# Two samples' steps dealt from a table, a gate's convolutions moved to VectorE, shorter checks, and q and k first in the ending

## The chip, the cores and the metric

The kernel runs on one core of a Trainium2 chip. A core has TensorE (PE, matrix products into the eight banks of PSUM), VectorE (DVE), ScalarE (ACT), GpSimd (POOL) and the queues that issue DMAs, here almost all SyncE's (SP). The metric is the device time of one execution in microseconds (us); several executions are made and their median is quoted. The profile is one further execution, taken by the hardware profiler.

## The reference

Sixteen samples x of 256 channels and 32 x 32 pixels, in float32, go through four layers (B the sample, C = 256, N = 1024 pixels):

```python
# layer 0: group norm, attention over pixels, projection, residual
xn = group_norm(x)
q, k, v = split(w_qkv @ xn + b_qkv)
x = w_proj @ (softmax(q.T @ k / sqrt(C)) @ v) + b_proj + x
# layer 1: a spatial gate
m, M = mean(x, channels), max(x, channels)
r = relu(conv3x3([m, M], w1) + b1)
x = x * sigmoid(conv3x3(m + M + r, w2) + b2)
# layer 2: like layer 0, with its own weights
# layer 3: attention with q and k of 32 channels, no norm
e = clip(q.T @ k / sqrt(32), -10, 10)
x = gamma * (softmax(e) @ v) + x
```

## The kernel before, in words

**Products.** The large products are made by Strassen's scheme in Winograd's form: `seven` takes 2 x 2 blocks and makes seven products instead of eight, with sums of blocks made by VectorE and results copied out of PSUM by ScalarE or added by VectorE (L909 plus, L978 and L1227 copies). Every float32 product is two passes on TensorE, so the profile counts two records for each. Weights are folded at the start (`fold`): logits are x^T M x with M from the weights of q and k, and the weights of v and of the projection are one matrix.

**A sample** is a generator, `sample(b)`, which issues a few instructions, yields, and goes on when it is called again. `attend` (layers 0 and 2) makes t = M x (`seven`, 4 yields), values (4), their sums (1), and for each half of the queries logits (8), a pause (2) and weighted values (7): 43 steps. Between layers 0 and 2 come 9 steps of waiting, the gate (`gate_of`, 4), the scaling of each half, its turn by VectorE and its way through DRAM into the channel layout (`turn` L825, `send` L836 and L840; 2), 4 of waiting, and the group norm (16). Then `attend` again, 7 of waiting, and layer 3 (`clipped_attend`, 30). That is 158 steps in all. Layer 3 has q and k by `qk_products` (L1375, on half the array's columns) and scores by `score_products` (L1401, four products at a time on 32 rows each; a group of them fills four banks and is emptied by four exponentials, L1417). A sample visits the scores four times. Even samples are lane 0, odd ones lane 1, each with its own buffers; the tile `t` of a lane holds t, then z (the turned gate result), then layer 3's q and k.

**The gate.** The planes of mean and maximum (pl, 128 x 8) are copied into 32 x 32 rows (L468), which `neighbours` (L458, L459) repeats on 96 partitions, shifted by one pixel. A convolution is then a product with a banded matrix `toep` (L473 for two planes, L490 for their sum). POOL builds `toep` at the start from a table of taps that is loaded (`build_toep`, L397 to L402; `tidx`, L582). The sigmoid is an exponential (L502), a sum and a reciprocal.

**The checks.** The fast path counts conditions on the data and weights in `n_ok`, and a general path runs if one fails. `alike` and `moderate` square weights, sum them over partitions by products with ones (L1103, L1147, L1157) and compare the extremes.

**The order.** Three generators are dealt out by a rule: `stream(0)` and `stream(1)` run even and odd samples one after another, and `later` holds the rest of the preparation (the head of sample 1, the folding of layers 2 and 3, `toep`, the checks). For `OFFSET` = 30 turns stream 0 alternates with `later`; after that the two streams alternate, `later` between them. The order in which the generators issue products is the order on TensorE. For the other engines `Plan` models each instruction's time and reorders each engine's queue by when its results are needed; `pin` fixes the planned order. Buffers of a pool are given out in the order of issue.

**The ending.** Sample 15's layer 3 is `ending`, written out by hand: the first value products, q and k, the other value products between scores, two halves of weighted values, and the output. It begins when stream 0 is done.

Of the kernel before, what the change touches and what calls it, by code (L numbers as in the profile page):

```python
# [41 lines left out]
OFFSET = 30  # L42
ROUNDS = 3
# [23 lines left out]
RESTART, ENTRY, MARGIN = 102, 93, 1.04  # L67
# [39 lines left out]
def durations(engine, ins, outs, reads, mode):  # L107
# [4 lines left out]
    if engine == PE:  # L112
        n = elements(reads[0].ap)
        if ins.is_transpose:
            return 110, 287
        if mode:
            return {"rows": (135, 496), "columns": (253, 403), "corner": (121, 210)}[mode]
        return max(224, 1.66 * n + 8), max(287, 0.84 * n + 178)
# [26 lines left out]
class Plan:  # L145
# [79 lines left out]
    def run(self, rank):  # L225
# [31 lines left out]
        def ready(i):  # L257
# [5 lines left out]
            for name in s.tiles:  # L263
                if name not in placed:
                    r = room(name)
                    if r is None:
                        return None
# [3 lines left out]
        def place(i, t):  # L271
# [13 lines left out]
            if s.engine == PE:  # L285
                more = RESTART * (t > free[PE] > 0)
                if s.mode != mode:
                    t, more = (t + ENTRY, more) if s.mode else (t, RESTART)
# [9 lines left out]
        for _ in range(n):  # L298
# [5 lines left out]
            for e in (DVE, ACT, POOL, SP):  # L304
                times = [(max(free[e], r), i) for i in waiting[e] for r in [ready(i)] if r is not None]
                if times:
                    t = min(times)[0]
                    i = min((rank[i], i) for u, i in times if u <= t + 1)[1]
                    if best is None or t < best[0]:
# [49 lines left out]
class Const:  # L359


    def __init__(self, nc, pool, vecs, scal):
# [15 lines left out]
        self.toep = pool.tile([P, 2 + NG, STRIP], FP, name="toep")  # L378
# [8 lines left out]
    def build_toep(self, tc, work, tidx):  # L387

        nc = tc.nc
        for k in range(3):  # L390
            for tap in range(9):
                w = self.sc[:, S_W1 + 9 * k + tap : S_W1 + 9 * k + tap + 1]
                if tap == 0:
                    one = self.toep[:, k, :]
                else:
                    one = work.tile([P, STRIP], FP, tag="tap", name=f"tap_{k}_{tap}")
                nc.gpsimd.tensor_scalar(one, tidx, float(tap), w, ALU.is_equal, ALU.mult)  # L397
                if tap:
                    nc.gpsimd.tensor_tensor(self.toep[:, k, :], self.toep[:, k, :], one, ALU.add)
            yield  # L400
        for g in range(1, NG):
            nc.gpsimd.tensor_copy(self.toep[:, 2 + g], self.toep[:, 2])  # L402
        nc.vector.tensor_scalar(self.neg_b2, self.sc[:, S_B2 : S_B2 + 1], -1.0, None, ALU.mult)
        yield
# [50 lines left out]
def neighbours(nc, rows):  # L455

    own, before, after = (rows[i * STRIP : (i + 1) * STRIP] for i in range(3))
    nc.vector.tensor_copy(before[..., 1:], own[..., :-1])  # L458
    nc.scalar.copy(after[..., :-1], own[..., 1:])  # L459


def gate_of(nc, k, small, psum, ptag, pl, rows, nm):

    for g in range(NG):
        copy = nc.scalar.copy if g % 2 else nc.vector.tensor_copy
        copy(rows[:STRIP, :2, g * NT : (g + 1) * NT], pl[g * STRIP : (g + 1) * STRIP])  # L468
    neighbours(nc, rows[:, :2])
    c1 = psum.tile([P, HALF], FP, tag=ptag, name=f"c1_{nm}")  # L470
    wide = k.toep.rearrange("p g j -> p (g j)")
    for i in range(2):
        nc.tensor.matmul(  # L473
            c1[:, :STRIP],
            wide[:, i * STRIP : i * STRIP + P],
            rows[:, i, :],
            start=(i == 0),
            stop=(i == 1),
        )
    r1 = small.tile([STRIP, STRIP], FP, tag="r1", name=f"r1_{nm}")  # L480
    nc.vector.tensor_scalar(
        r1, c1[:STRIP, :STRIP], k.sc[:STRIP, S_B1 : S_B1 + 1], 0.0, ALU.add, ALU.max
    )
    yield None
    inner = rows[:STRIP, 2, :]
    nc.vector.tensor_tensor(inner, rows[:STRIP, 0, :], rows[:STRIP, 1, :], ALU.add)
    nc.vector.tensor_tensor(inner, inner, r1, ALU.add)
    neighbours(nc, rows[:, 2])
    c2 = psum.tile([P, HALF], FP, tag=ptag, name=f"c2_{nm}")
    nc.tensor.matmul(  # L490
        c2[:, :STRIP],
        k.toep[:, 2:, :].rearrange("p g j -> p (g j)"),
        rows[:, 2, :],
        start=True,
# [1603 lines left out]
```

## Time and profile before

| | us |
|---|---|
| runs | 2644.03, 2646.5, 2647.04 |
| median of the runs | 2646.5 |
| profiled execution | 2642.92 |
| its span | 2641.1 |
| TensorE busy, of the span | 2622.2 |
| VectorE busy | 2143.3 |
| ScalarE busy | 1349.1 |

The span runs from the first instruction's start to the last one's end; the profiled execution's own time is 1.8 us longer. A group line of the profile names the line of the kernel, the engine, the operation, what it writes and reads, its shape and the count; then busy us in total, the mean duration in ns, and the engine's idle time ahead of it with what ended it. A timeline line has the start in us, a length, the engine and the line, for runs of like instructions. Neighbours overlap in it, since the ends of matmuls are modelled; the time that a group takes is read from start to start.

### The profile page before, as it was taken

The page shows a single profiled execution, that of the slowest core. Times are in us where ns is not written, and L with a number is a line of the kernel's source. Part 1 is how long each engine was busy: PE and PEld are TensorE (multiplying, and loading weights), DVE is VectorE, ACT ScalarE, POOL GpSimd, SP SyncE. Part 2 cuts the span into 40 slices and gives each one's busy share as a digit, 9 for nine tenths or more (in the row PEclk, how much of TensorE's full clock was granted, in tenths as well). Part 3 has the DMA queues.
Part 4 walks back from the last instruction along what each step waited for, and adds up shares of the span by engine and source line. Part 5 has one row for each costly group of instructions (what it writes and reads, how often), then busy time and mean ns, then how long its engine had stood idle before and what let it go on. Part 6 is the DMA issues. An engine that isn't in the chain of part 4 may idle for free.

```text
span 2641.1 us, 47888 instructions
## 1 busy us (share of the span) xinstructions
PE 2622.2 (99%) x18998; PEld 2368.0 (90%) x18998; DVE 2143.3 (81%) x4180; ACT 1349.1 (51%) x2825; POOL 69.7 (3%) x172
## 2 busy tenths in 40 slices
PE   8999999999999999999999999999999999999998
PEld 7888899888988989989889898998989989899897
DVE  8798887988778887788877888778887788878776
ACT  5454455544565445554555545555455544545453
POOL 5000000000000000000000000000000000000000
PEclk9999999999999999999999999999999999999999
DMA  4021211112121120211201212112111121101111
GB/s 118 1 65 49 57 33 37 53 49 65 25 57 49 41 73 9 57 56 41 65 17 49 65 33 65 32 34 65 49 49 33 33 65 49 49 17 33 49 39 44
DMA packets 135878, 123.08 MB, mean 47 GB/s; under 512 B 12768, under 2 KB 126688, under 8 KB 135648
## 3 DMA queue, kind: packets, MB, share of 16 engines
q1 hardware_dynamic: 133776, 118.76, 16.4%
q8 instruction: 153, 2.51, 0.4%
q10 hardware_dynamic: 1872, 1.18, 0.1%
q14 instruction: 77, 0.63, 0.1%
HBM read 69.58 MB, written 50.33 MB: 45 GB/s over the span
## 4 chain that ended last, share of the span: by engine, by line
PE 98%; DVE 1%; ACT 0%; DMA 0%; issue 0%; SPq 0%; DVEq 0%; ACTq 0%
PE b_l L877 19%; PE af_l L877 13%; PE c_l L877 13%; PE sb_l L877 13%; PE sc_l L877 8%; PE vb_l L877 5%; PE sf_l L877 4%; PE sa_l L877 4%; PE vc_l L877 3%; PE tb_l L877 3%; PE s L1401 3%; PE tc_l L877 2%; PE vf_l L877 2%; PE va_l L877 1%; PE tf_l L877 1%; PE qk L1375 1%
## 5 line engine op out<-in xcount | busy, mean ns | idle before, releaser
L877 PE MATMUL sb_l<-t_l,x 128*128 128x256 f32 x1024 | 256.9, 381 | 0.0
L877 PE MATMUL b_l<-vt,e_l 128*128 128x128 f32 x2048 | 250.2, 275 | 0.0
L877 PEld LDWEIGHTS b_l<-vt,e_l 128*128 128x128 f32 x2048 | 242.6, 192 | 4.9 <-issue 2.3
L988 ACT ACTIVATE e_l<-e_l 128x512 f32<-128x512 f32 x256 | 160.4, 630 | 119.0 <-DVE e_l L909 118.4
L877 PEld LDWEIGHTS sb_l<-t_l,x 128*128 128x128 f32 x1024 | 185.0, 190 | 31.8 <-issue 10.3
L978 ACT COPY e_l<-sb_l 128x512 f32<-128x512 f32 x256 | 149.1, 583 | 103.9 <-PE sb_l L877 102.3
L909 DVE TENSOR_TENSOR e_l<-sc_l,e_l 128x512 f32<-128x512 f32 x128 | 88.2, 689 | 119.2 <-PE sc_l L877 94.2
L877 PE MATMUL c_l<-tv,cb_l 128*128 128x129 f32 x1504 | 184.0, 275 | 0.0
L1417 ACT ACTIVATE e<-s 128x512 f32<-128x512 f32 x256 | 133.8, 601 | 97.0 <-PE s L1401 96.1
L909 DVE TENSOR_TENSOR e_l<-sb_l,e_l 128x512 f32<-128x512 f32 x256 | 172.9, 683 | 9.6 <-PE sb_l L877 5.0
L877 PEld LDWEIGHTS c_l<-tv,cb_l 128*128 128x128 f32 x1504 | 176.7, 191 | 0.8
L990 ACT ACTIVATE e_l<-e_l 128x1024 f32<-128x1024 f32 x128 | 135.2, 1056 | 76.2 <-DVE e_l L909 76.0
L793 ACT ACTIVATE xr<-xr,bstrip 128x128 f32<-128x128 f32 (+1 forms) x376 | 141.5, 437 | 16.2 <-DMA xr<-in_x_dram 10.2
L877 PE MATMUL sf_l<-tc_l,x 128*128 128x256 f32 x512 | 132.4, 381 | 0.0
L877 PE MATMUL sc_l<-tc_l,xs_l 128*128 128x256 f32 x512 | 131.6, 379 | 0.0
L877 PE MATMUL sa_l<-t_l,x 128*128 128x256 f32 x512 | 131.4, 379 | 0.0
L877 PE MATMUL sc_l<-t_l,xs_l 128*128 128x256 f32 x512 | 131.4, 379 | 0.0
L877 PE MATMUL sb_l<-tc_l,xs_l 128*128 128x256 f32 x512 | 131.4, 379 | 0.0
L877 PE MATMUL af_l<-vt,e_l 128*128 128x128 f32 x1024 | 127.2, 277 | 0.0
L877 PEld LDWEIGHTS af_l<-vt,e_l 128*128 128x128 f32 x1024 | 119.4, 192 | 8.1 <-issue 8.1
L877 PE MATMUL b_l<-tv,e_l 128*128 128x128 f32 x1024 | 125.7, 275 | 0.0
L877 PE MATMUL c_l<-vt,e_l 128*128 128x129 f32 x1024 | 125.4, 275 | 0.0
(304 smaller groups left out, 5840.6 us busy)
## 6 DMA issues: line engine op xcount, KB each, us to landing
x<-mid_x SPq DMA_DIRECT2D x64, 512.0 KB, 3.6
xr<-in_x_dram SPq DMA_DIRECT2D x64, 256.0 KB, 5.0
mid_x<-t_z SPq DMA_DIRECT2D x128, 128.0 KB, 2.3
mid_x<-t_l SPq DMA_DIRECT2D x128, 128.0 KB, 2.3
x<-in_x_dram SPq DMA_DIRECT2D x62, 256.0 KB, 3.8
out_dram<-xr SPq DMA_DIRECT2D x124, 128.0 KB, 2.3
raw_l<-in_w_l_dram SPq DMA_DIRECT2D x1, 1024.0 KB, 6.8
raw_l<-in_w_l_dram SPq DMA_DIRECT2D x2, 256.0 KB, 4.3
```

Source lines behind the costliest of these rows:

```text
L793: nc.scalar.activation(y[:, s, ts], y[:, s, ts], AF.Identity, bias=bias[:, s : s + 1])
L877: mm = nc.tensor.matmul(out, left, right, start=fresh and m == 0 and (lone or i == 0), stop=(m == len(pairs) - 1), skip_group_check=True,)
L909: nc.vector.tensor_tensor(dst, src, dst, ALU.add)
L978: nc.scalar.copy(block(i, j), ps.rearrange("p (m n) -> p m n", m=2))
L988: nc.scalar.activation(part, part, AF.Exp)
L990: nc.scalar.activation(e[:, m : m + 2, :], e[:, m : m + 2, :], AF.Exp)
L1375: nc.tensor.matmul(ps[i * PH : (i + 1) * PH, : qt * P].rearrange("p (g n) -> p g n", g=qt), w3qk[:, c, i], xt[:, g0 : g0 + qt, c], start=( ...
L1401: nc.tensor.matmul(ss[g][:, j * 2 * P : (j + 1) * 2 * P].rearrange("p (t g j) -> p t g j", t=TPH, g=2), qk[gs, mh, 1 - blk, j * P : (j + 1 ...
L1417: nc.scalar.activation(by_strip[:, :, :, qa], ss[g].rearrange("p (m t n) -> p m t n", m=2, t=TPH), AF.Exp,)
```

## The change

The turns come from a table: `FIRST_TURNS`, four times `TURNS`, `LAST_TURNS`, each digit one step of stream 0, stream 1 or `later` (2). `TURNS` has 316 digits, 158 for each stream. The planner's constants and some of its rules change with it. The gate's convolutions are made by VectorE on 32 partitions: products of nine shifted views with nine taps, a reduction, a 32 x 32 turn, and another reduction; `toep`, `tidx` and the loads of the tap table go, and the scratch lies in z, which is taken before the gate now. In the checks POOL adds the halves first, and one product is made where there were two or three. In the weighted values a reciprocal moves up. The ending begins with q and k, copies a column of sums with the result instead of reading it from PSUM, and makes the product of s3 of its second half behind that of s4.

```diff
-OFFSET = 30
-ROUNDS = 3
+FIRST_TURNS = (
+    "22222000020000000200200200000001000002002022122221002022221110000122022222222222000"
...
+TURNS = (
+    "10000110001110010000001001001001111111111111111111111000101000111111100001101110"
+    "01001000101000110011101111100100101000100010010000000000100000000000000000001000"
+    "01000011011111000111111111111111001111000111100101111000010010100010000000111111"
+    "0110010011110000110110011111111011100001000001001101101111110100010111101111"
+)
...
+CYCLES = 4
+ROUNDS = 4
...
-RESTART, ENTRY, MARGIN = 102, 93, 1.04
+RESTART, ENTRY, EXIT, MARGIN = 102, 190, 205, 1.04
+AHEAD = 1000
...
-            return {"rows": (135, 496), "columns": (253, 403), "corner": (121, 210)}[mode]
+            return {"rows": (108, 496), "columns": (216, 403), "corner": (121, 210)}[mode]
...
-                    if r is None:
+                    if r is None or self.users[name][0] != i:
...
-                    t, more = (t + ENTRY, more) if s.mode else (t, RESTART)
+                    t, more = (t + ENTRY, more) if s.mode else (t, EXIT)
...
+                    late = t + steps[i].issue
+                    soon = [
+                        (rank[j], u, j)
+                        for u, j in times
+                        if t + 1 < u < late and rank[j] < rank[i] and 1 < rank[j][0] < late + AHEAD
+                    ]
+                    if soon:
+                        _, t, i = min(soon)
...
+def spread(ap, *steps):
+    return bass.AP(ap.tensor, ap.offset, [list(ap.ap[0])] + [list(step) for step in steps])
+
+def convolved(nc, k, planes, first, flip, turned, taps, part, out):
+    for i, plane in enumerate(planes):
+        w = k.sc[:STRIP, first + 9 * i : first + 9 * (i + 1)]
+        nc.vector.tensor_tensor(
+            taps[:, 3 * i : 3 * (i + 1)],
+            spread(plane, (1, 3), (0, 3), (1, STRIP)),
+            spread(w, (1 if flip else 3, 3), (3 if flip else 1, 3), (0, STRIP)),
+            ALU.mult,
+        )
+    nc.vector.tensor_reduce(part, taps[:, : 3 * len(planes)].rearrange("p t d r -> p d r t"), AX.X, ALU.add)
+    nc.vector.transpose(turned[:, :, 1 : 1 + STRIP], part)
+    row = turned.shape[-1]
+    nc.vector.tensor_reduce(
+        out, spread(turned[:, 0, 0:1], (1, STRIP), (row + 1, 3)), AX.X, ALU.add
+    )
...
+    nc.vector.tensor_tensor(
+        total, rows[:STRIP, 0, inside], rows[:STRIP, 1, inside], ALU.add
     )
+    nc.vector.transpose(total_t, total)
+    planes = [rows[:STRIP, i] for i in range(2)]
+    convolved(nc, k, planes, S_W1, False, rows[:STRIP, 3:6], taps, part, c1)
     yield None
...
+    nc.vector.tensor_scalar(c1, c1, k.sc[:STRIP, S_B1 : S_B1 + 1], 0.0, ALU.add, ALU.max)
+    nc.vector.tensor_tensor(rows[:STRIP, 2, inside], c1, total_t, ALU.add)
+    convolved(nc, k, [rows[:STRIP, 2]], S_W2, True, rows[:STRIP, 6:9], taps, part, c2)
     yield None
...
             nc.scalar.copy(acc[:, hi, P:], c)
+            nc.vector.reciprocal(ri[:, n1 : n1 + 2], acc[:, hi, C])
             yield
...
-            nc.vector.reciprocal(ri[:, n1 : n1 + 2], acc[:, hi, C])
             go(s3, t3, b, fresh=False)
...
+            nc.gpsimd.tensor_tensor(sq[:, :C], sq[:, :C], sq[:, C:], ALU.add)
             yield from pause()
             ps = bank(f"size_{nm}")
...
+            nc.tensor.matmul(ps[:, :C], k.ones, sq[:, :C], start=True, stop=True)
...
+            flat = dg.rearrange("p c n -> p (c n)")
+            for part in (sq[:, C:], flat):
+                nc.gpsimd.tensor_tensor(sq[:, :C], sq[:, :C], part, ALU.add)
             yield from pause()
...
+            nc.tensor.matmul(ps[:, :C], k.ones, sq[:, :C], start=True, stop=True)
...
+            z = slot("t", lane, [P, NH, NG, C], f"z_{b}")
+            free = z[:STRIP].rearrange("p h b n -> p (h b n)")
+            gate = gate_of(nc, k, small, pl, rows[lane], free, f"l1_{b}")
...
+                pss = [qk_products(h) for h in range(NH)]
+                qk_copies(0, pss[0])
                 vb_ps, va_ps = bank("vb_end"), bank("va_end")
...
-                pss = [qk_products(h) for h in range(NH)]
-                qk_copies(0, pss[0])
...
-                keep(hi, c2, c_ps[:, :, :P])
-                nc.vector.reciprocal(ri[:, 2:4], c_ps[:, :, P])
+                keep(hi, slice(P, C + 1), c_ps)
+                nc.vector.reciprocal(ri[:, 2:4], acc[:, hi, C])
...
-                go(s3, t3, b_ps, fresh=False)
-                keep(hi, c1, b_ps)
-                plus1(hi, c2, b_ps)
-                plus1(hi, c1, af[:, 1])
-
...
                 count(ri, f"l3_{b}")
+                go(s3, t3, b_ps, fresh=False)
+                keep(hi, c1, b_ps)
+                plus1(hi, c2, b_ps)
+                plus1(hi, c1, af[:, 1])
+                for i in range(2, 4):
+                    done(i, slice(0, C))
...
-        streams = [stream(0), stream(1)]
-        rest = later()
-        for _ in range(OFFSET):
-            next(streams[0])
-            next(rest, None)
-        for _ in in_turn([in_turn(streams), rest]):
+        streams = [stream(0), stream(1), later()]
+        for turn_of in FIRST_TURNS + CYCLES * TURNS + LAST_TURNS:
+            next(streams[int(turn_of)], None)
+        for _ in in_turn(streams):
             pass
```

## The prediction

> **What bounds the kernel now.** Page part 1 first, then the chain.
>
> ```profile
> span 2641.1 us, 47888 instructions
> PE 2622.2 (99%) x18998; PEld 2368.0 (90%) x18998; DVE 2143.3 (81%) x4180; ACT 1349.1 (51%) x2825; POOL 69.7 (3%) x172
> PEclk9999999999999999999999999999999999999999
> PE 98%; DVE 1%; ACT 0%; DMA 0%; issue 0%; SPq 0%; DVEq 0%; ACTq 0%
> ```
>
> TensorE (PE) is busy 99% at full clock and carries 98% of the chain. So a microsecond off its queue is a microsecond off the end, while VectorE (DVE, 81%) and ScalarE (ACT, 51%) can take work as long as PE doesn't come to wait for it. A busy share hides pauses under modelled ends, so I read starts: sixteen 128-column passes take 1.79 us (775.09 to 776.88 below), and a pause is what the next start lies beyond that. The idle 19 us lie in the first 40 us, the last 60 and the tail; the table by stretches has 199.95 to 200 of each 200 us between.
>
> PE's groups by line, then its timeline at an even sample's gate, an odd one's, and a group of layer 3's scores (start, length of the run of records, line; the last number is the count of passes):
>
> ```profile
> L473 PE MATMUL c_l<-rows,toep 128*128 128x32 f32 x64 | 9.3, 269 | 0.4
> L490 PE MATMUL c_l<-rows,toep 128*128 128x32 f32 x32 | 4.9, 236 | 0.0
> L1103 PE MATMUL size_l<-sq_l,ones 128*128 128x256 f32 x12 | 3.1, 380 | 0.0
> L1147 PE MATMUL reach_l<-msq_l,ones 128*128 128x256 f32 x8 | 2.1, 380 | 0.0
> L1157 PE MATMUL reachb_l<-mdg_l,ones 128*128 128x256 f32 x4 | 1.2, 379 | 0.0
> ```
>
> ```profile
> 772.86 0.53 PE L473 MATMUL c_l<-rows,toep 128*128 128x32 f32 x4
> 773.22 2.03 PE L877 MATMUL c_l<-tv,cb_l 128*128 128x129 f32 x16
> 775.09 1.95 PE L877 MATMUL b_l<-tv,e_l 128*128 128x128 f32 x16
> 776.88 0.31 PE L490 MATMUL c_l<-rows,toep 128*128 128x32 f32 x2
> 777.02 2.03 PE L877 MATMUL c_l<-vt,e_l 128*128 128x129 f32 x16
> ...
> 812.17 1.06 PE L877 MATMUL va_l<-wvp_l,x 128*128 128x128 f32 x8
> 813.27 0.63 PE L473 MATMUL c_l<-rows,toep 128*128 128x32 f32 x4
> 813.74 1.14 PE L877 MATMUL vc_l<-vc_l,xs_l 128*128 128x128 f32 x8
> ...
> 911.10 1.95 PE L877 MATMUL b_l<-vt,e_l 128*128 128x128 f32 x16
> 912.97 1.15 PE L1401 MATMUL s<-t_qk 32*128 32x256 f32 x16
> 914.05 1.13 PE L877 MATMUL sb_l<-t_l,x 128*128 128x256 f32 x4
> ```
>
> **The change part by part.** *Gate.* An even sample's first convolution moves the next product by 0.36 us (772.86 to 773.22), its second by 0.14. An odd one's first lies in 1.57 us (812.17 to 813.74), 0.89 of it the eight passes of va (as 814.72 to 815.61): 0.68, with 0.2 of waiting for the planes; its second 0.14. That is 1.32 us a pair, 8 pairs: **-10.6**. (The busy sums, 9.3 + 4.9, count ends that overlap the neighbours.)
>
> VectorE takes over. Per sample the new gate has on 32 partitions a sum (0.17, as L486), a 32x32 turn (0.2, as L418), two products of 288 elements (0.45 each: L948 takes 0.42 for 256), a reduction of 576 (0.75, between L1113's 0.41 for 256 and L1301's 1.21 for 1024), a turn of 96 (0.28; L427's 64 take 0.24) and a reduction of 96 (0.27); then 0.20 + 0.17 for bias and sum, one product of 288 (0.45), a reduction of 288 (0.45), 0.28 and 0.27: 4.4 us. Gone are L458 twice, L481, L486, L487: 0.94. Net +3.45, 55 us in all, and DVE comes to some 2195 us, 84% of the new span. I cost it at nothing, covered by the other stream's products; without that cover it is the second rival. Two ACT copies (L459, 0.23 each) go, so no one waits for those. The chain itself gets no longer: now rows leaves at 767.0 and sg stands at 779.8, much of that waiting for the convolutions' places in PE's order.
>
> *Checks.* 24 passes of 256 columns become 10; four such passes start 0.86 apart (915.02 to 915.88), so 14 x 0.216 = **-3.0**. The seven additions on POOL are 256 elements each, about 0.9 us by L600 (0.46 to 0.64 for 128), and lie in place of some 23 us of POOL's work on the band tables (L397, L399, L402). What queues behind them on POOL are rstd (L437) and the counts; the four steps of pause before each check cover them. Five DVE copies and two additions (0.42 each) go.
>
> *Startup.* Three loads of tidx leave SP's queue (11.26 to 13.26), so qb and xr start up to 2 us sooner; PE waits for neither. The new turns put two sets of layer 2's transposes ahead of the first sample's first product, which now starts at 16.08 after waiting 2.0 for x. Layer 2's weights are issued at 10.08 and take 6.8 to land: 16.9. So 0.8 is lost, while the gaps between 16.1 and 21.7 (1.8 us) can fill. Bounds -1 and +1, taken 0.
>
> *Turns: score visits.* A sample has 158 steps: 43 for each of two attentions, 9 before the gate, 4 in it, 2 for scaling, 4, 16 for the norm, 7, and 30 for layer 3. Laying the tables' digits over them gives PE's order, since products stay in program order. Samples 0 to 14 visit the scores in 60 separate places now; by the tables two groups of one sample stand side by side in 21 cases (39 places; 3 mergers in each cycle of TURNS). One visit costs 914.05 - 911.10 - 1.79 = 1.16 us. Its sixteen passes run four at a time; inside it the bursts start at 0, 0.32, 0.54 and 0.75, so at pace it would need 4 x 0.215 = 0.86, and 0.30 is for going in and out. No merged visit is in this trace: bounds 0 and 0.30 each; I take 0.30, since the third and fourth burst follow at pace within one visit: 21 x 0.30 = **-6.3**. The Trainium skill, TensorEngine Tiling (Array Packing), Key Properties, says that changing the tiling mode drains TensorE; by that rule two groups in one mode pay once, and the trace's 0.30 per visit agrees.
>
> *Turns: handovers.* Where an odd sample goes from layer 2 to layer 3, its sums must go through DRAM before q and k. The table leaves there two weighted products (2 x 1.79), seven t products (7 x 0.86) and two value products (2 x 0.89): 11.4 us, in five of the pairs, more in the others. Now an odd sample's last product ends at 956.86, its load is issued at 966.21 and lands 3.6 later (part 6), at 969.8: 12.9 us, with other DVE work (L1056) between the two turns (L825, 959.49 and 961.77). An even one's ends at 885.14, issue 893.27, landing 896.9: 11.7. With the two additions (L909) that stood in its way on DVE gone it would be 10.5. So 0 to 1.5 each; nearest is the even one, whose turns follow each other: 0.35 x 5 = **+1.7**. From layer 0 to layer 2 the table leaves an even sample two halves of logits and weighted products of the other (12.0 + 12.5 each: 49 us, where 760.6 to 805.3 are 45 now) and an odd one a whole attention (61, where 45 now). No wait is added there.
>
> *Ending.* PE's waits in the last 66 us:
>
> ```profile
> PE s L1401 <- DVE t_qk L1394: 1.7, 2, 0.9
> PE b_end L877 <- ACT acc_end L1500: 0.5, 1, 0.5
> PE c_end L877 <- DVE ri L1573: 0.2, 1, 0.2
> ```
>
> With q and k ahead of the first value products the copies (DVE 0.49 each, six; ACT the rest) get 1.78 us more, for 1.7 of waiting. Sums copied to acc let go of c's bank without the reciprocal; the product of s3 behind s4 gives b's copy 1.8 us. All three go: **-2.4**. Late next may be q and k themselves: x's second half now is issued at 2587.81, landing about 2591.4 by the median, and they start at 2591.07; seven weighted products then lie ahead where there are six and two value products, the same 12.5 us. Scaling moved behind s3 (0.9 us of DVE) fits under the last product (1.8). Bounds -0.5 and -2.4.
>
> *Sum* against the profiled execution (2642.9, its span 2641.1): -10.6 - 3.0 - 6.3 + 1.7 - 2.4 = -20.6, 2622.3. The median of the runs, 2646.5, lies 3.6 above that execution; runs are what I forecast, so most of that is added: **2625**.
>
> **The rivals.** *Banks run out at merged visits.* Two groups side by side fill all eight PSUM banks, and ACT empties one per 0.52 us (L1417: 133.8 us for 256). The first is free about 0.8 us after the first group, 0.2 before the second ends, if ACT stands ready; behind another exponential (L990, 1.06) PE waits 0.8, and with the other stream's three banks still full it waits in the middle. At 0.6 each, 12.6 us: 2638, the mergers worse than nothing. For it speaks that layer 0's and 2's products follow at once and need a bank; against it, ACT's 51%. The skill's same page, PSUM Bottleneck, warns that tiling speeds up TensorE and not the emptying of PSUM; this rival is that rule at work here.
>
> *DVE is full at the gates.* Its rows between 810 and 850 are 9.23, 9.61, 9.43 and 9.55 of 10: 2.2 us free in 40, and there the odd samples' gates lie; 3.45 more doesn't fit in the old stretch. If PE waits for all that is added, 55 us come back: 2680, slower. It decides from 24.5/16 = 1.3 to 1.5 us a sample on. Against it: the stretch grows from 45 to 61 us, DVE's busy 42.8 of 45 becoming about 57 of 61 by its other work; the even one has 10 us free (37.76 of 48). If only odd samples pay, 8 x 3.45 gives 2652.
>
> *The turns change nothing*, because visits stay apart or pay in full: 2625 + 6.3 - 1.7 = 2630.
>
> **How the numbers follow.** Forecast 0.62 (its own range 2616 to 2634: startup 1, handovers 0 to 7.5, ending 2), banks 0.12, turns 0.06, DVE 0.20. A measurement here tells 0.2%, 5 us, from no change. DVE's case spreads from 2640 to 2680: 0.05 still faster, 0.06 the same, 0.09 slower. The other cases are faster, but for 0.02 of the banks' at double price, split evenly. So faster 0.83, same 0.07, slower 0.10. The range, 2614 to 2650, leaves out 0.12 above and some 0.05 below.
>
> **What would show it.** Right: no L473 or L490 of PE; the chain still 98% PE; score groups of 32 passes taking some 2.0 us; DVE near 2195 busy; no wait of L1401 in the ending. Wrong: PE waiting for ACT at e<-s behind merged scores, for x at q and k, or for x after group norm; stretches of 200 us with PE under 199.

## The result and the profile after

The kernel after the change takes 2620.7 us (median of four runs, 2617.1 to 2623.1) against 2646.6 (2644.0 to 2647.0) for the kernel before, measured beside it: a ratio of 0.9906, 95% interval 0.9892 to 0.9920. The profiled execution took 2623.14 us with a span of 2621.4, so 19.8 us left the span (2641.14 less 2621.37). The medians of the runs lie 25.9 us apart: before's profiled execution is 3.7 us under its median, after's is the slowest of its four runs, 2.4 above. What follows places the 19.8 us; no trace here divides the other 6. (The first line of FIRST_TURNS in the diff above has wrong digits; in the kernel it reads `22222000020000000200200000001000002002022122221002022221110000122022222222222000`.)

The head of the page and the shares of the chain, of after:

```profile
span 2621.4 us, 47843 instructions
PE 2600.0 (99%) x18888; PEld 2359.2 (90%) x18888; DVE 2199.2 (84%) x4301; ACT 1337.3 (51%) x2793; POOL 60.4 (2%) x124
...
PE 96%; DVE 1%; DMA 1%; SPq 0%; ACT 0%; issue 0%; ACTq 0%
```

TensorE is still the bound. It has 110 instructions fewer: 96 of the gate, 14 of the checks. VectorE has 56 us more, as forecast. All waits of TensorE that the profile names, of after (us in total, times, longest):

```profile
PE wtp_l L642 <- DMA raw_l<-in_w_l_dram: 8.5, 2, 4.9
PE strips_l L718 <- DVE bcol L710: 1.7, 1, 1.7
PE vc_l L898 <- DVE t_qk L1397: 1.2, 5, 0.2
PE af_end L898 <- DVE acc_end L1506: 0.9, 1, 0.9
PE af_l L898 <- ACT e_l L1009: 0.8, 2, 0.4
PE fold_l L654 <- ACT wt_l L648: 0.2, 1, 0.2
```

There is none at L1404 any more (the ending's wait for t_qk), none for x at q and k, and none for x behind the group norm. New are a second wait for weights and one for bcol at the start, five short ones at L898 behind VectorE's copies of q and k, two at af_l for ScalarE's e_l, and af_end.

Summing, over all of TensorE's instructions, how far the next start lies beyond the pace of its shape places the 19.8 us: first start +0.2; first 45 us +2.2; products that are gone -13.7 at nominal pace; the rest, up to the last weighted product of layer 2 ahead of the ending's q and k, -6.1; the ending from there on -2.2; tail -0.2. The sum is -19.8.

The score visits, in after's timeline of TensorE (start, length of the run, line, count of passes last):

```profile
905.00 1.95 PE L898 MATMUL b_l<-vt,e_l 128*128 128x128 f32 x16
906.88 2.10 PE L1404 MATMUL s<-t_qk 32*128 32x256 f32 x32
908.92 1.13 PE L898 MATMUL sb_l<-t_l,x 128*128 128x256 f32 x4
909.88 1.03 PE L898 MATMUL sa_l<-t_l,x 128*128 128x256 f32 x4
```

Two groups side by side take 2.04 us from start to start, and the runs around them are longer by 0.09 (1.88 for 1.79) and 0.10 (0.96 for 0.86): 2.23 in all. A single group takes 1.17 with the same 0.10 behind it, 1.27. A merger therefore saves 2 x 1.27 - 2.23 = 0.31.

The start, in TensorE's timeline and in the stretches of after (busy us per engine, then the granted clock, the share of the DMA engines, GB/s):

```profile
16.29 0.41 PE L718 MATMUL strips_l<-bcol,ident 128*32 128x2 f32 x8 [1.68 <-DVE bcol L710]
20.29 1.97 PE L642 MATMUL wtp_l<-ident,raw_l 128*128 128x128 f32 x8 [3.59 <-DMA raw_l<-in_w_l_dram]
22.05 1.71 PE L898 MATMUL tb_l<-x,m_l 128*128 128x512 f32 x2
```

```profile
15.00:20.00 5.00, 0.41 (x8) 0.33 (x8) 2.24 (x12) 1.52 (x2) 1.09 (x3) 0.66 1.00 239
20.00:25.00 5.00, 4.71 (x14) 3.12 (x15) 2.71 (x9) 0.69 (x1) 1.23 (x4) 0.66 0.67 157
```

Layer 2's weights, which the table now puts ahead of the first sample, were issued at 10.76 and landed at 20.25: 9.5 us, for 6.8 before, with the DMA engines full at that time. TensorE stands 3.59 us, and its clock is 0.66 in these two rows.

This is one execution's start and not the table's price. Four kernels below have the same table and the same loads in the same order (gate_x2, gate_x3, gate_late, spare_products). There the weights landed in 6.3 to 7.2 us, TensorE waited 0.3 to 1.0 us for them, and by the same sums the first 45 us are 2.5 to 4.3 us shorter than after's, which is 0.3 to 2.1 us shorter than before's. In spare_products:

```profile
16.82 1.09 PE L650 MATMUL wtp_l<-ident,raw_l 128*128 128x128 f32 x8 [0.63 <-DMA raw_l<-in_w_l_dram]
```

The slow clock is not new either. In before it follows eight one-column products (13.16) and a pause of 1.97 us:

```profile
15.00:20.00 5.00, 3.92 (x13) 1.64 (x14) 3.85 (x15) 2.21 (x3) 3.31 (x8) 0.66 0.49 159
```

### The profile page after: what moved, and what is told of

It reads as the page before. It is cut to its first block, busy times and chain, and to the rows that moved or that the text cites. A ratio compares the mean times of both kernels' runs of the same rounds, so it can differ in the third digit from the quotient of the medians.

```text
span 2621.4 us, 47843 instructions
## 1 busy us (share of the span) xinstructions
PE 2600.0 (99%) x18888; PEld 2359.2 (90%) x18888; DVE 2199.2 (84%) x4301; ACT 1337.3 (51%) x2793; POOL 60.4 (2%) x124
## 4 chain that ended last, share of the span: by engine, by line
PE 96%; DVE 1%; DMA 1%; SPq 0%; ACT 0%; issue 0%; ACTq 0%
PE b_l L898 19%; PE af_l L898 13%; PE c_l L898 13%; PE sb_l L898 12%; PE sc_l L898 8%; PE vb_l L898 4%; PE sf_l L898 4%; PE sa_l L898 4%; PE tb_l L898 3%; PE vc_l L898 3%; PE s L1404 2%; PE tc_l L898 2%; PE va_l L898 1%; PE vf_l L898 1%; PE qk L1378 1%; PE tf_l L898 1%
## 5 line engine op out<-in xcount | busy, mean ns | idle before, releaser
L898 PE MATMUL sb_l<-t_l,x 128*128 128x256 f32 x1024 | 256.9, 382 | 0.0
L898 PE MATMUL b_l<-vt,e_l 128*128 128x128 f32 x2048 | 250.7, 275 | 0.0
L898 PEld LDWEIGHTS b_l<-vt,e_l 128*128 128x128 f32 x2048 | 242.3, 192 | 7.4 <-issue 2.8
L898 PEld LDWEIGHTS sb_l<-t_l,x 128*128 128x128 f32 x1024 | 187.2, 190 | 29.6 <-ACT e L1420 5.0
L930 DVE TENSOR_TENSOR e_l<-sb_l,e_l 128x512 f32<-128x512 f32 x256 | 171.3, 681 | 19.8 <-PE sb_l L898 14.1
L898 PE MATMUL c_l<-tv,cb_l 128*128 128x129 f32 x1504 | 183.2, 274 | 0.0
L898 PEld LDWEIGHTS c_l<-tv,cb_l 128*128 128x128 f32 x1504 | 175.5, 191 | 0.1
L1011 ACT ACTIVATE e_l<-e_l 128x1024 f32<-128x1024 f32 x128 | 135.2, 1056 | 62.3 <-DVE e_l L930 61.4
L1081 ACT COPY acc_l<-c_l 128x258 f32<-128x258 f32 x94 | 35.4, 376 | 216.9 <-PE c_l L898 216.9
L898 PE MATMUL sc_l<-tc_l,xs_l 128*128 128x256 f32 x512 | 131.7, 380 | 0.0
L898 PE MATMUL sf_l<-tc_l,x 128*128 128x256 f32 x512 | 131.5, 379 | 0.0
L898 PE MATMUL sc_l<-t_l,xs_l 128*128 128x256 f32 x512 | 131.4, 379 | 0.0
L898 PE MATMUL sb_l<-tc_l,xs_l 128*128 128x256 f32 x512 | 131.4, 379 | 0.0
L898 PE MATMUL sa_l<-t_l,x 128*128 128x256 f32 x512 | 131.4, 379 | 0.0
L898 PE MATMUL af_l<-tv,e_l 128*128 128x128 f32 x1024 | 125.3, 275 | 0.8 <-ACT e_l L1009 0.8
L898 PE MATMUL af_l<-vt,e_l 128*128 128x128 f32 x1024 | 125.0, 275 | 0.0
L898 PE MATMUL c_l<-vt,e_l 128*128 128x129 f32 x1024 | 124.9, 275 | 0.0
```

The lines of the kernel that those rows point to most:

```text
L898: mm = nc.tensor.matmul(out, left, right, start=fresh and m == 0 and (lone or i == 0), stop=(m == len(pairs) - 1), skip_group_check=True,)
L930: nc.vector.tensor_tensor(dst, src, dst, ALU.add)
L1011: nc.scalar.activation(e[:, m : m + 2, :], e[:, m : m + 2, :], AF.Exp)
L1081: nc.scalar.copy(acc[:, hi, P:], c)
```

## The experiments

One pause decides most of what follows, so it is named here. Between a sample's last weighted product of layer 0 and its Bt products of layer 2 lies a chain: last sums, channel maximum (pl), gate, sigmoid (sg), scaling, turns, a way through DRAM, group norm, x. Meanwhile TensorE works through the other sample's products in the order of the turns. I call the time of those products the cover, and the time from the last weighted product to the end of L465 (x normed) the chain. For odd samples both are counted from the even sample's Bt products, which follow that last weighted product at once or, where TensorE stalls, behind the stall. In before, cover and chain are 44.7 and 44.4 us for even samples and 45.6 and 40.1 for odd ones. In after they are 49.2 and 48.5, and 61.5 to 62.1 and 57.4 to 60.4. An even sample's handover in before, on VectorE and on TensorE:

```profile
804.16 0.80 DVE L446 TENSOR_SCALAR x<-x,a_l,bb_l 128x1024 f32<-128x1024 f32 x1
805.27 1.02 PE L877 MATMUL tb_l<-x,m_l 128*128 128x512 f32 x2
```

and in after, on TensorE and on VectorE:

```profile
797.78 1.95 PE L898 MATMUL b_l<-vt,e_l 128*128 128x128 f32 x16
799.56 1.02 PE L898 MATMUL tb_l<-x,m_l 128*128 128x512 f32 x2
```

```profile
798.06 0.79 DVE L465 TENSOR_SCALAR x<-x,a_l,bb_l 128x1024 f32<-128x1024 f32 x1
```

x is ready at 798.86, and TensorE takes it at 799.56 without a pause. The margin of an even sample was small already: 0.3 us in before, 0.7 now.

**The old turns** (turns_old):

```
-        streams = [stream(0), stream(1), later()]
-        for turn_of in FIRST_TURNS + CYCLES * TURNS + LAST_TURNS:
-            next(streams[int(turn_of)], None)
-        for _ in in_turn(streams):
+        streams = [stream(0), stream(1)]
+        rest = later()
+        for _ in range(30):
+            next(streams[0])
+            next(rest, None)
+        for _ in in_turn([in_turn(streams), rest]):
```

> The changed kernel with the old rule of turns (30 turns of stream 0 with the rest, then alternating); gate on VectorE, checks, ending and planner as changed. Theory (the turns' gain is the score visits that stand together, 6.5 us by the trace after, less some 3 us of new waits and of a startup that waits for layer 2's weights): some 3 to 5 us above the changed kernel's 2621, 64 score visits in the trace, and no wait of TensorE in the pairs, so the gate's gain stands without the table. Rival (the old turns leave too little room for VectorE, which is 94 to 96% busy around the odd samples' gates): the table is what makes the gate on VectorE pay, TensorE waits around 810 to 850 in every pair, and the time comes to 2635 or more.

Measured: 2707.0 us, ratio 1.0230 (1.0216 to 1.0244), 86 above after where a few were expected. Its timeline of TensorE at an odd sample, and its first wait:

```profile
863.23 1.03 PE L898 MATMUL sa_l<-t_l,x 128*128 128x256 f32 x4
868.76 2.05 PE L898 MATMUL tb_l<-x,m_l 128*128 128x512 f32 x2 [4.50 <-issue]
870.60 1.91 PE L898 MATMUL ta_l<-x,m_l 128*128 128x512 f32 x2
```

```profile
PE tb_l L898 <- issue: 55.0, 16, 6.7
```

x was normed at 868.65, so "issue" is x. All sixteen stalls stand at this one place: 1.3 to 1.7 us at even samples, 4.5 to 6.7 at odd ones, and behind the long ones two passes of 512 columns take 1.84 us where they take 0.86. The chain takes 45.4 to 45.8 and 49.3 to 51.5 us for a cover of 44 and 44.7. So the largest part of the table's worth is not the mergers: under the old rule the new gate costs more than it saves.

**The old gate** (gate_old): after's table, with neighbours, gate_of, build_toep and the loads of tidx as in before.

> The changed kernel, its table of turns too, with the gate's convolutions back on TensorE as banded products. Theory: the gate costs TensorE 13.2 us in all: 10.6 as forecast and 0.08 more on the run of products behind each of the 32 gate products; so 2634, and 2632 or less if the trailing 0.08 is an error of the records. Rival: VectorE's relief gives part of it back, 5 us or more, and the time stays under 2629.

Measured: 2811.0 us, ratio 1.0624 (1.0609 to 1.0638). TensorE's first two waits:

```profile
PE tb_l L911 <- DVE x L480: 91.7, 7, 14.1
PE c_l L507 <- DVE rows L492: 32.7, 6, 5.4
```

One pair, the rows on VectorE and then the convolutions and the Bt products on TensorE:

```profile
798.13 0.18 DVE L492 COPY rows<-rows 32x62 f32<-32x62 f32 x1
```

```profile
837.57 0.53 PE L507 MATMUL c_l<-rows,toep 128*128 128x32 f32 x4
848.42 1.03 PE L507 MATMUL c_l<-rows,toep 128*128 128x32 f32 x4 [5.44 <-DVE rows L492]
863.27 2.05 PE L911 MATMUL tb_l<-x,m_l 128*128 128x512 f32 x2 [12.24 <-DVE x L480]
```

The expectation fell. The even sample's rows are there at 798.3, but the table deals its first convolution so late that TensorE comes to it at 837.57, 39 us afterwards (in before 4.1 us: 768.8 to 772.86); its chain takes 71 us, and x comes 11 to 14 us late in seven of the eight pairs and 7.6 in the first. The odd sample's first convolution stands right behind its last weighted product, and TensorE waits 5.4 us for its rows. Gate and table belong together: either alone is slower than before.

**More work for VectorE at the gate** (gate_x3, and later gate_x2 with REPEAT = 2):

```
+REPEAT = 3
...
-    for i, plane in enumerate(planes):
+    for i, plane in [p for _ in range(REPEAT) for p in enumerate(planes)]:
...
-    nc.vector.tensor_reduce(part, taps[...], AX.X, ALU.add)
+    for _ in range(REPEAT):
+        nc.vector.tensor_reduce(part, taps[...], AX.X, ALU.add)
```

> The changed kernel with the tap products and their reduction of each gate convolution made three times over (same results): some 5.1 us more of VectorE per sample, 80 in all, VectorE near 2280 us. Theory (the other stream's products cover it, with room): within 3 us of the changed kernel. Rival (VectorE is full at the gates): every microsecond that is added there comes back in TensorE's waits, 40 to 80 us more, 2660 to 2700.

> The kernel after with the products of the taps and the sums over them done twice: 2.55 us more of VectorE's time per sample, half of what gate_x3 added. Theory (cover): the room of 7.3 and 4.3 us takes it, even where the chain grows by twice that because its later steps now meet the other sample's sums on VectorE: no stall of TensorE at the normalization or one under 1 us per pair, 2619 to 2630 us. Rival (VectorE full, as the prediction had it, with a break-even at 1.3 to 1.5 us more per sample): 2.55 - 1.4 = 1.15 us at each of 16 samples, 2639 us or more.

Measured: gate_x3 2723.8 us, ratio 1.0295 (1.0281 to 1.0309); gate_x2 2638.6 us, 0.9975 (0.9965 to 0.9985), so 103 and 18 us above after. TensorE in gate_x3, around an even sample's handover:

```profile
821.08 1.95 PE L902 MATMUL b_l<-vt,e_l 128*128 128x128 f32 x16
833.51 2.05 PE L902 MATMUL tb_l<-x,m_l 128*128 128x512 f32 x2 [10.48 <-issue]
835.35 1.91 PE L902 MATMUL ta_l<-x,m_l 128*128 128x512 f32 x2
```

and in gate_x2 its waits at the same line:

```profile
PE tb_l L902 <- issue: 10.3, 8, 1.3
PE tb_l L902 <- PE b_l L902: 5.3, 7, 0.8
```

With 5.1 us more per sample the even chain grows from 48.5 to 60.1 us: 10 us of stall in each pair. The 103 us are more than all the work that was added (some 80), and its stalls are all at even samples. While TensorE stands, VectorE is busy for 10.05 of 10.40 us (823.0 to 833.4), so gate_x3 alone does not tell lateness from a full VectorE. With 2.55 it grows to 50.5, against a cover of 49.2 (1.3 of stall), and the odd one to 62.3 against 61.5 (0.8): 15.6 of the 18 us. Both expectations that spoke for "no stall" fell. In after x is normed only 0.7 us before its even Bt products, and mostly 3.1 to 3.6 before its odd ones. I had counted 7.3 and 4.3 us of room for it from the landing of the data, which was wrong: VectorE does other work in between. The rival's number for gate_x2 came out to within 0.4 us; the next run shows that its reason was not needed.

**A longer chain without more work on VectorE** (gate_late):

```
+LINKS = 10
...
+    for _ in range(LINKS):
+        nc.gpsimd.tensor_copy(part, part)
     nc.vector.transpose(turned[:, :, 1 : 1 + STRIP], part)
```

> The kernel after with ten copies of 32x96 numbers onto themselves on GpSimd, one behind the other, put between each convolution's sum over the taps and its transpose: nothing is added to VectorE, but the gate's chain becomes longer by some 20 x 0.4 = 8 us per sample. Theory (cover): in the kernel after the data of the even sample land 7.3 us earlier than its Bt products would need them (786.10 plus 6.15 for the last statistics and the normalization against 799.57), those of the odd one 4.3 us; 8 us more length then give a stall of 0.7 to 2 us at each even and of about 4 us at each odd sample, with some 2 us of slow passes behind the longer one: 6 to 8 us per pair, 2660 to 2690 us. Rival (VectorE is the bound once its work at the gate grows): its work is unchanged, 2617 to 2625 us.

Measured: 2730.9 us, ratio 1.0327 (1.0308 to 1.0346), more than expected. GpSimd's copies in the timeline of gate_late, then VectorE's rows behind the first ten:

```profile
785.74 3.12 POOL L496 COPY t_z<-t_z 32x96 f32<-32x96 f32 x10 [8.13 <-DVE t_z L522]
797.08 3.46 POOL L496 COPY t_z<-t_z 32x96 f32<-32x96 f32 x10 [8.22 <-DVE t_z L494]
```

```profile
789.36 1.22 DVE L1030 TENSOR_TENSOR cb_l<-e_l 128x1024 f32<-128x1024 f32 x1
790.62 1.22 DVE L1031 TENSOR_TENSOR e_l<-e_l 128x1024 f32<-128x1024 f32 x1
791.95 1.23 DVE L1076 TENSOR_TENSOR e_l<-cb_l,e_l 128x1024 f32<-128x1024 f32 x1
...
793.74 1.22 DVE L1082 TENSOR_TENSOR e_l<-e_l 128x1024 f32<-128x1024 f32 x1
794.88 0.26 DVE L497 STREAM_TRANSPOSE rows<-t_z 32x96 f32<-32x96 f32 x1
```

Ten copies were done at 788.86, but their successor on VectorE, L497, stands at 794.88, behind five sums of the other sample; the second ten end at 800.54 and theirs stands at 807.13. The copies take 6.6 us per sample, yet sg comes 15.7 us later (38.4 us behind the last weighted product, for 22.7). The orders of the engines are fixed beforehand by the planner's prices, and its price for such a copy on GpSimd, 460 + 2 x 96 = 652 ns to the next and 832 to its completion, is twice the 329 measured and more. That would let the planner put other work ahead of a step that was in truth ready; no run here has the price put right. TensorE stalls 11.8 us in each pair at the even samples. VectorE has 15.5 us more busy time than in after (2214.7), 81% of the span, and 48.0 of the 61 us of such a stretch, so "VectorE is full" is not needed for a loss of 110 us; lateness is enough.

**Both parts undone** (both_old): gate_old's gate and turns_old's turns in one kernel; the checks, the ending and the planner's numbers stay.

> The kernel after with two parts undone together: the old rule for the turns and the gate's convolutions on TensorE. What is left of the change is the checks by one product, the ending that begins with q and k, the planner's new numbers. Theory now (cover): TensorE keeps the order of the turns, so between the end of the channel maximum and the Bt products of layer 2 lies a fixed stretch of the other sample's products; the old rule makes it 39.5 us for the even and 39.6 us for the odd samples, and the chain from the maximum to the end of the normalization takes 39.2 and 34.1 us with the convolutions on TensorE (before) but 40.4 and 46.3 us with them on VectorE under the same rule (turns_old). So with both undone nothing stalls, and the gain is checks 3.0 and ending 2.5: 2646.6 - 5.5 = 2641 us, 2639 to 2644. Rival (the planner's new numbers, not the gate, spoil the old rule): the stalls of turns_old stay, 2680 to 2707 us.

Measured: 2640.1 us, ratio 0.9981 (0.9972 to 0.9990) to a before of 2645.0 on this chip: 5.0 us less, as expected. The stalls of turns_old are gone (chains 44.4 and 40.1 us again), so the planner's new numbers did not make them. Where the gain lies is less clear than its sum: the checks account for 3.0, and by the starts of TensorE the first 45 us are shorter by 2.0, but its pauses behind 2560 us grew from 6.7 to 10.4 in the profiled execution, which was the slowest of its eleven runs. Under the old turns the ending gained nothing in that execution.

**The gate's small products, without their dependencies** (spare_products): per sample two products at the first convolution's place and one at the second's, of constants, into a bank that nobody reads.

```
+    for i in range(count):
+        nc.tensor.matmul(
+            ps[:, :STRIP], k.ones, k.ident[:, :STRIP], start=(i == 0), stop=(i == count - 1)
+        )
```

> The kernel after with the gate's TensorE work put back without its dependencies: per sample two products of 128 rows by 32 columns at the first convolution's place and one at the second's, of constants, into a bank that nobody reads. It measures by itself what the removal was worth on TensorE. The prediction's step said 32 visits for 10.6 us; the starts in the record of before give 13.2 us, since the run behind each small product is longer by 0.08 us. By the second the kernel is 13 us slower than after (2634 us), by the first 10.6 us slower (2631 us); if most of the price in before was waiting for the planes, under 6 us (2621 to 2627 us).

Measured: 2628.3 us, ratio 0.9939 (0.9924 to 0.9954), 7.6 above after and between the cases that were expected. The products come in 18 places, mostly six passes together. By the starts, six passes take 0.59 us and the run behind them 0.08 more, which sums to 10.7 us over the kernel; the start of this kernel is 4.3 us shorter than after's (its second wait for weights is 0.6 us, not 3.6), and after's two waits at af_l are not there (1.2), so the spans of the profiled executions differ by only 4.8. The products with the runs behind them thus cost 10.7 us, and the 13.2 that I read from before holds 2.5 us of something else. It is in before's weight loads, at each odd sample:

```profile
813.27 0.52 PEld L473 LDWEIGHTS c_l<-rows,toep 128*128 128x128 f32 x4 [0.24 <-ACT rows L459]
```

There TensorE waited for the rows, and an odd sample's first visit is 0.31 us longer than an even one's: 8 x 0.31 = 2.5.

**The old rule with another lead** (offset_40, offset_36, both_old_40): turns_old, and both_old, with 40 or 36 instead of 30 in the loop.

> The kernel after without the table: again the old alternating rule, but with 40 turns ahead for the even sample instead of 30. Counted along TensorE's order with the durations of one product from the trace (0.86 us for 512 columns, 0.432 for 256, 0.224 for 128), the stretch between the last weighted product of layer 0 and the Bt products of layer 2 grows from 44.05 to 49.1 us for the even samples and from 44.7 to 50.1 us for the odd ones; turns_old took 45.4 to 45.8 and 49.3 to 51.4 us for what has to be done in it. Theory (cover): the stalls of turns_old (8 x 8.2 us, and the slow passes behind them) are gone but for 0 to 1 us per odd sample, and the kernel is both_old (2640 us) less the 13.2 us that the gate's products cost on TensorE: 2627 us, 2622 to 2635 us. Rival (the gate on VectorE pays only with the table's order, because VectorE's other work stands in its way): 2660 us or more.

> As offset_40 with 36 turns ahead: the stretch is 50.1 us for the even and 49.06 us for the odd samples, which needed 49.3 to 51.4 us in turns_old. Theory (cover): no stall at the even samples, 0.2 to 2.3 us at each odd one, so up to 19 us more than offset_40: 2628 to 2648 us, with the waits at the Bt products of odd samples alone. Rival (VectorE in the way): 2660 us or more.

> both_old (convolutions on TensorE, alternating rule) with 40 turns ahead instead of 30. Its stretch grows from 44.3 and 44.9 to 49.3 and 50.3 us, but both_old has no wait there that could go. Theory (cover): the same time as both_old within 4 us, 2636 to 2644 us; the longer stretch has no worth of its own. Rival (the larger lead is itself faster, for instance by fewer meetings on VectorE): 2633 us or less.

Measured: 2693.1 us, ratio 1.0178 (1.0161 to 1.0195); 2681.8, 1.0137 (1.0116 to 1.0157); 2687.5, 1.0158 (1.0141 to 1.0175). All three expectations fell. The largest waits of offset_40 and then of both_old_40:

```profile
PE tb_l L898 <- issue: 25.8, 8, 3.5
PE qk L1378 <- DMA x<-mid_x: 9.3, 1, 9.3
```

```profile
PE tb_l L911 <- issue: 20.6, 7, 3.3
PE qk L1390 <- DMA x<-mid_x: 9.1, 1, 9.1
```

The cover grew as counted, and the odd samples no longer stall. But the even chain grew with it: to 53.2 us in offset_40 and to 52.5 to 53.4 in both_old_40, where the gate is the old one and the chain took 44.4 with a lead of 30. A chain thus has no fixed length of its own: with the same gate it changes with the order of the turns. That it depends on which of the other sample's sums share VectorE with it is what the next run asks. offset_36 stalls at both samples (27.2 us in 11 waits). The larger lead also leaves the last sample's way to q and k uncovered (9 us). For even samples, one pair each:

| kernel | VectorE busy in the stretch | chain | cover |
|---|---|---|---|
| before | 35.9 | 44.4 | 44.7 |
| turns_old | 40.0 | 45.4 | 44 |
| after | 41.6 | 48.5 | 49.2 |
| gate_x2 | 44.1 | 50.5 | 49.2 |
| both_old_40 | 46.7 | 53.4 | 50 |
| offset_40 | 49.2 | 53.2 | 49.5 |
| gate_late | 48.0 | 61.1 | 49.2 |

A longer stretch holds more of VectorE's work whatever its cause, so the first two columns of numbers rise together in part by themselves; as a share of the stretch VectorE is busy 80% in before, 92% in offset_40 and 79% in gate_late, and that does not order the chains.

**Less of the other sample's work on VectorE** (fewer_sums): turns_old with

```
-            plus(1, 1, b)
-            plus(1, 0, b)
+            if not less:
+                plus(1, 1, b)
+                plus(1, 0, b)
```

and less set for the scores of layers 0 and 2.

> turns_old (old alternating rule with 30 turns ahead, convolutions on VectorE) without the last two of the five sums that VectorE makes for each group of scores of layers 0 and 2; this leaves part of the scores out, and TensorE's products and their order stay as they were. Each stretch between the last weighted product of layer 0 and the Bt products of layer 2 (44.05 and 44.7 us of the other sample's products) holds four such groups, so 4 x 2 x 0.60 = 4.8 us of VectorE's time leave it, and none of what the gate itself needs. Theory now (the time the chain takes is not its own length but goes with VectorE's whole work in the stretch, 88 and 90% busy in turns_old): the chain falls from 45.4-45.8 and 49.3-51.4 us by about 4.8 us, the even samples' stall (1.6 us) is gone, the odd ones' (5.2 us) falls to 0 to 2 us: 2707 less 8 x 6.5 us less most of the slow passes behind (8 x 3 us), 2630 to 2655 us. Rival (the chain's own steps, its transfers and waits set its length, whatever VectorE does for the other sample): the stalls stay, 2690 us or more.

Measured: 2683.0 us, ratio 1.0145 (1.0128 to 1.0162), between the two. Its two stretches, even and odd, and its first wait:

```profile
768.90:812.80 43.90, 43.90 (x313) 41.63 (x313) 34.38 (x77) 23.65 (x56) 0.69 (x1) 1.00 0.17 49
812.90:861.70 48.80, 44.73 (x275) 38.65 (x274) 42.25 (x96) 26.46 (x53) 0.89 (x2) 1.00 0.22 66
```

```profile
PE tb_l L898 <- issue: 36.0, 8, 5.2
```

VectorE's busy time in the even stretch (the third engine figure) fell from 40.0 to 34.4, the chain from 45.4 to 43.3, and the stall is gone. In the odd stretch it fell only from 44.6 to 42.3, and the chain stayed at 48.8 to 49.9, with a stall of 4.3 to 5.4. So for even samples the other sample's sums are a part of the chain's length (5.6 us less of VectorE's work, 2.1 us less of chain), and for odd ones it was not settled what sets it: VectorE has pauses in it (6.5 of 48.8 us), and the gate from pl to sg still takes 19.1 us, for 10.9 with the convolutions on TensorE.

**A table with a mended start** (mended): the first digits deal the loads of the first samples later, and the last a(0,1) product gets a bank of its own.

```
-    "22222000020000000200200000001000002002022122221002022221110000122022222222222000"
+    "20000222220000000200200000001000002002022122221002022221110000122022222222222000"
...
-                go(a(0, 1), vb(1, 0), af[:, 0])
+                own = bank("own_end")[:, : 2 * P].rearrange("p (i c) -> p i c", i=2)
+                go(a(0, 1), vb(1, 0), own)
...
-                    scaled(to, af[:, 0, i], h * TPH + i, to)
+                    scaled(to, own[:, i], h * TPH + i, to)
```

> The changed kernel with two edits: the first sample's four t steps dealt ahead of layer 2's transposes (first digits 2 0000 2222 2 instead of 22222 0000 2), and the last product before the output into a bank of its own. Theory: TensorE's wait of 3.6 us for layer 2's weights at 16.7 to 20.3 goes, with the slower clock behind it, and the 0.9 us wait for the sum read from the shared bank: 3 to 5 us less, 2616 to 2618. Rival: the first sample's products wait for the normalised x and its sums instead, and the output's tail is set by VectorE: 0 to 1 us.

Measured: 2619.1 us (2618.3 to 2620.1), ratio 0.9898 (0.9883 to 0.9913). The span is 2617.5, 3.9 below after's, and 3.0 of that are in the first 45 us, where the wait of 3.59 is gone. That the new digits did this is not shown: spare_products, with after's digits, has a start that is 1.3 us shorter still, and the weights landed in 6.4 us there and in 6.5 here. The bank brought nothing: the wait at af_end went, TensorE waits 0.5 at the next place, and the ending's pauses are 3.8 us for 3.7. In the runs the two intervals overlap, so mended is not shown to be faster than after; it is the fastest of all kernels here by its span.

## Why the prediction held, step by step

Forecast were 2625 us from a sum of -20.6; measured are 2620.7 and -19.8 in the profiled executions. The sum is right partly by luck, because errors cancel. The 4.3 us between 2625 and 2620.7 come mostly from what was added for the distance of the median from the profiled execution: before's median lies above it, after's below.

- *Gate, -10.6 forecast.* Measured -13.2. The term that was missing is the run behind each of the 32 visits, longer by 0.08: 2.6 us. That spare_products comes to 10.7 is luck: it holds the visits and those runs (8.0 + 2.6) without waits, while the forecast's 10.6 holds the visits and the odd samples' longer first visit (8.0 + 8 x 0.32), 0.2 of which was put down to the planes.
- *"The chain itself gets no longer."* This step failed. From pl to sg the chain took 14.0 and 10.9 us, and takes 18.3 and 21.0; it is a dozen dependent steps on VectorE, each behind some of the other sample's sums. I had put the old 14 us down to the convolutions' places in TensorE's order. It cost nothing only because the table lengthens the cover to 49.2 and 61.5 us, which I had read rightly (49 and 61) but noted as an aside ("no wait is added there"). That sentence carried the forecast: turns_old shows 86 us behind it, of which the mergers are 6.5. That 49.2 us suffice for a chain of 48.5 was worked out nowhere in the prediction; as far as the forecast goes it is luck.
- *VectorE full at the gates.* It did not come. The busy time forecast for the odd stretch, 57 of 61, is 55.6 of 61.5; the even one has 7.6 us free of 49.2, for the 10 forecast, and still only 0.7 us to spare, since free time in the stretch is not slack of the chain. The break-even of 1.3 to 1.5 us of waiting per sample was near: in gate_x2, 2.55 us more of VectorE's work cost 18 us, 1.1 per sample.
- *Checks, -3.0.* Right.
- *Startup, 0 within 1.* In the profiled execution +2.2: I took 6.8 us for the landing of layer 2's weights from before, and there they took 9.5. In the four kernels with the same start they took 6.3 to 7.2, and the first 45 us are 0.3 to 2.1 us shorter than before's, so the term fits those but for one that is beyond its lower bound.
- *Score visits, -6.3.* Measured -6.5 for 21 mergers. The Trainium skill (TensorEngine Tiling (Array Packing), Key Properties) states that a change of the tiling mode drains TensorE; that two groups in one mode then pay once agrees with the trace, 0.31 per merger. Late next are five single visits behind which TensorE each time waits some 0.3 us for VectorE's copies of q and k: +1.5.
- *Banks run out.* It did not come: a merged visit runs through in 2.04 us, in 20 of 21 places. Not foreseen are two waits at af_l for ScalarE's e_l: +1.3 by the starts.
- *Handovers, +1.7.* Measured 0: no wait for x at q and k in after.
- *Ending, -2.4.* The waits named did go; by the starts they and their restarts come to 3.3. New is af_end, 1.1 us with its restart, because both af products share a bank and VectorE still reads the first: -2.2 remains.

These terms sum to -19.9, against -19.8. The mechanism "nothing on TensorE's path waits for the new work on VectorE" is shown by after's list of waits; that 0.7 us were left at even samples was not foreseen.

## What to carry to other kernels

Before work is moved from the bounding engine to one with idle time, find the chain that the moved steps lie in, and compare its length with the work the bounding engine has in its queue until it needs the result; a share of 84% said nothing about that here, and slack of the chain must be read at its last step, not at the landing of its data. A changed order of two streams is worth what it covers, so it is judged together with the chain that it was made for: here each of the two changes alone lost 60 to 165 us, and both together won 26, of which both_old gives 5 to the rest of the change. Where orders are fixed beforehand by estimated durations, a wrong estimate may delay a step by the estimate and not by what it takes; gate_late suggests this and does not prove it.

## What the hardware showed that was not expected

A long pause of TensorE costs more than itself. After 4.50 us (turns_old) and 10.48 us (gate_x3) of standing, the next passes of 512 columns started 0.92 us apart instead of 0.43 for some 3.5 us, at a granted clock of 0.50 as the stretch behind the pause in gate_x3 shows:

```profile
833.50:837.00 3.50, 3.49 (x4) 1.49 (x5) 3.50 (x5) 0.69 (x1) 0.00 (x0) 0.50 0.00 0
```

That adds about 2 us to each. After 1.29 us (gate_x2) the clock stayed at 1.00. The nine kernels that stall at the Bt products of layer 2 have 90 such pauses behind 100 us, counted from start to start:

| pause, us | pauses | added to the next ten passes, us |
|---|---|---|
| up to 2.5 | 31 | 0.1 or less |
| 2.7 to 3.5 | 12 | 1.2 to 1.8 in eight, 0.1 in four |
| 3.6 and more | 47 | 1.5 to 3.1 |

The Trainium skill, TensorE: Matmul & The Clock Gate, in its part on the HAM clock gate, gives an idle window of about 3.4 us after which the clock is halved, and about as much busy time to restore it. Most of these pauses agree; those from 2.7 to 3.5 us that slowed the passes are partly shorter, and in before's start 1.97 us behind one-column products was enough (0.66).

A small product also costs the run behind it: 0.08 us behind products of 32 columns, 0.10 behind a visit to the 32-row scores, although the passes themselves are at pace again.
